# C for a state-space scan in sixteen copies in memory, one for each eight partitions, in a four-layer convolution kernel

## The chip, the core and the metric

The kernel runs on one core of one Trainium2 chip. A core has a matrix engine (PE in the profile, its weight loads shown as PEld), a vector engine (DVE), a scalar engine (ACT), a general engine (POOL) and a queue engine (SP) that here only issues DMAs. Sixteen DMA engines, shared by all queues of the core, move data between the chip's memory and the on-chip memory of 128 partitions (rows). The metric is the time of one launch in device microseconds.

## What is computed

The input is a tensor of 16 images with 192 channels of 64 x 64 points. Four residual layers follow each other, each of the form x = x + layer(groupnorm(x)): an elementwise likelihood model (layer 0), a five-point stencil with a 960-to-192 matrix (layer 1), a selective scan (layer 2), and a depthwise convolution with a batch norm (layer 3). The change is in layer 2:

```python
xs = jnp.stack([xf, xt, xf[..., ::-1], xt[..., ::-1]], axis=1)   # 4 directions k
x_dbl = jnp.einsum('bkdl,kcd->bkcl', xs, x_proj_weight)
dts, Bs, Cs = jnp.split(x_dbl, [R, R + N], axis=2)               # N = 16 states, R = 6
...
def step(h, inp):
    d, u, Bt, Ct = inp
    dA = jnp.exp(d[..., None] * A)
    h = dA * h + (d * u)[..., None] * Bt[:, :, None, :]
    y = jnp.einsum('bkdn,bkn->bkd', h, Ct)
    return (h, y)
```

For each image b, direction k and state n, C is one row of 4096 values, and it multiplies the state of every one of the 192 channels. B is used the same way.

## The kernel before

**Tiles.** Two images make a pair, and a pair's 384 rows (2 x 192 channels) are three tiles j of 128 partitions. Tile 0 holds rows of the first image only, tile 2 rows of the second only, and tile 1, the middle one, 64 rows of each. Eight pairs are worked off one after the other by `pair`: `scans` (layer 2) and then `layer3`. Inside the scans of pair i, the generator `front` does layers 0 and 1 and the projections of layer 2 for pair i+1, a little at each step, on whatever engines have room. The front of the first pair runs alone, before any scan.

**The scan loop.** `scans` runs 768 steps s a pair: over the tiles j, in each over the four directions in the order `ORDER` = (1, 3, 0, 2), in each over four chunks of `LC` = 1024 points, in each over the 16 states n. A step is: PE spreads one row of B over 128 partitions (`spread`), DVE multiplies it by du (`product`), ACT makes dA (`decay`), DVE runs the recurrence (`TENSOR_TENSOR_SCAN` into `h`). Two states share a tile `h`[128, 2048]; after each second step u = s // 2 POOL multiplies that tile by `cb`, the two rows of C spread over all partitions (L1035). After each fourth step POOL also issues a DMA that adds one `h` tile to another (L1037, `h<-h` in the profile), and PE sums the result up over the states (`add_up`). There are five `h` tiles and three `cb` tiles; a scan that opens an `h` tile waits until the DMA and the sums that used it before are done.

**Where C comes from.** `project` makes B, C and dt for chunk c of 512 points. The 128 rows of C are 64 rows for k = 1, 3 (which need their columns and rows exchanged) and 64 for k = 0, 2, and all are written by one DMA into `c_d` (L759). `split` reads the first 64 back into `nat`, ACT exchanges them into `ct` (L830), and one DMA for each m puts `ct` into `cp_d` (L832). `load_c(u)` (L966), called at every second step for the step after the next (L1132), issues the DMA for `cb`: two rows of 1024 values of `c_d` or `cp_d` that lie side by side, read as one row of 8 KB by each of the 128 partitions (L977). For the middle tile it issues two DMAs of 64 partitions each, one for each image.

**Order.** In the scans the instructions stand in the order in which the program issues them (`_InOrder`). SP carries the `cb` loads, all loads and stores of the front, and the loads of B and dt; each of its DMAs signals through one of eight semaphores in turn and first waits for the DMA that had that semaphore before.

Of the kernel before, what the change touches and what calls it, by code (L numbers as in the profile page):

```python
# [22 lines left out]
P = 128  # L23
# [3 lines left out]
L = HW * HW  # L27
# [9 lines left out]
K, N, R = 4, 16, 6  # L37
LC = 1024
NC_ = L // LC
ORDER = (1, 3, 0, 2)  # L40
RD = 2 * R


SUM = 6

# [59 lines left out]
def conv_preact_kernel(ctx: ExitStack, tc: tile.TileContext, a: dict):  # L107
    nc = tc.nc
    x_in = a["x"]
    out = a["out"]  # L110
# [24 lines left out]
    for part in range(3):  # L135
        rows = slice(32 * part, 32 * part + 32)
# [162 lines left out]
    class Made:  # L299
        def __init__(self, n):  # L300
            def d(name, shape, dtype=F32):
                return dram.tile(shape, dtype, name=f"{name}{n}")

            self.x2 = d("x2_d", [NT * P, L])
            self.b = d("b_d", [P, L])
            self.c = d("c_d", [NC_, P, LC])
            self.dt = d("dt_d", [K * RD, L])

            self.bp = d("bp_d", [K, BP, L], BF16)
            self.cp = d("cp_d", [NC_, 2 * 2 * N, LC])  # L310
            self.dtp = d("dtp_d", [2 * RD, L])
            self.gm = const.tile([P, NT], F32, name=f"gm{n}")
            self.rstd = const.tile([P, NT], F32, name=f"rstd{n}")
            self.std = const.tile([P, NT], F32, name=f"std{n}")
# [322 lines left out]
    def layer1(o, E, ps, deep, st, gm, rstd):  # L637
        with tc.tile_pool(name="l1w", bufs=1) as w_, tc.tile_pool(name="l1x", bufs=2) as xk, tc.tile_pool(
# [87 lines left out]
                advance()  # L726
            yield

    def project(o, E, ps):

        with tc.tile_pool(name="pjw", bufs=1) as w_, tc.tile_pool(name="pjx", bufs=3) as xk:
            less = w_.tile([P, NT], F32, name="less")
            E.act.activation(less, o.gm, AF.Copy, scale=-1.0)
            proj = w_.tile([P, NT, 2 * P + K * RD], F32, name="projs")
            E.sp.dma_start(out=proj, in_=a["proj"])
            xns = {}

            def load(c):
                if c < 8:
                    xns[c] = xk.tile([P, NT, 512], F32, name="pj_x")  # L740
                    for j in range(NT):
                        E.sp.dma_start(
                            out=xns[c][:, j, :],
                            in_=row_tiles(o.x2)[:, j, 512 * c : 512 * c + 512],
                        )

            after = []

            def norm(c, j):
                if c < 8:  # L750
                    on_scalar(E, xns[c][:, j, :], xns[c][:, j, :], less, o.rstd, j)

            def done(to, c, m, p):
                yield
                yield
                r = xk.tile([P, 512], F32, name="pj_r", tag="pj_r")[:m]
                E.act.copy(r, p)
                cs = slice(512 * (c % 2), 512 * (c % 2) + 512)
                E.sp.dma_start(  # L759
                    out=to[c // 2, :, cs] if to is o.c else to[:, 512 * c : 512 * c + 512], in_=r  # L760
                )
                yield

            def advance():
                for g in list(after):
                    if next(g, after) is after:
                        after.remove(g)

            load(0)
            load(1)  # L770
            for _ in range(3):
                yield
            for j in range(NT):
                norm(0, j)
                yield
            for c in range(8):
                for at, (to, d0, m) in enumerate(
                    ((o.b, 0, P), (o.c, P, P), (o.dt, 2 * P, K * RD))
                ):
                    p = ps("pj_p")[:m]  # L780
                    for j in range(NT):
                        E.pe.matmul(
                            p, proj[:, j, d0 : d0 + m], xns[c][:, j, :], start=(j == 0), stop=(j == NT - 1)
                        )
                        yield 0.57
                        advance()
                    norm(c + 1, at)
                    after.append(done(to, c, m, p))
                xns.pop(c)
                load(c + 2)  # L790
            while after:
                yield
                advance()
            yield

    def split(o, E):

        with tc.tile_pool(name="sp1", bufs=1) as one, tc.tile_pool(name="sp2", bufs=2) as two:
            nat = one.tile([P, L], F32, name="nat")
            E.sp.dma_start(out=nat[0:64, :], in_=o.b[0:64, :])  # L800
            E.sp.dma_start(
                out=nat[64:128, :].rearrange("p (m l) -> p m l", l=LC),
                in_=o.c[:, 0:64, :].rearrange("m p l -> p m l"),
            )
            bts, dts = {}, {}

            def load(m):
                if m < NC_:
                    bts[m] = two.tile([P, LC], F32, name="bt")
                    E.sp.dma_start(out=bts[m][64:128, :], in_=o.b[64:128, LC * m : LC * m + LC])  # L810

            def load_dt(m):
                if m < NC_:
                    dts[m] = one.tile([2 * RD, LC], F32, name="dtn")
                    E.sp.dma_start(
                        out=dts[m].rearrange("p (h w) -> p h w", w=LC // HW),
                        in_=image(o.dt[: 2 * RD, :])[:, :, 16 * m : 16 * m + 16],
                    )

            load(0)  # L820
            load_dt(0)
            for _ in range(5):
                yield
            for m in range(NC_):
                load(m + 1)
                cs = slice(LC * m, LC * m + LC)
                bt = bts.pop(m)
                ct = one.tile([P, LC], F32, name="ct")
                for rows, to in ((slice(0, 64), bt), (slice(64, 128), ct)):
                    E.act.copy(image(to[rows, :]), columns(nat[rows, :])[:, 16 * m : 16 * m + 16, :])  # L830
                    yield
                E.sp.dma_start(out=o.cp[m], in_=ct[64:128, :])  # L832
                dt = one.tile([2 * RD, LC], F32, name="dtt")
                E.act.copy(image(dt), dts.pop(m).rearrange("p (h w) -> p w h", w=LC // HW))
                yield
                E.sp.dma_start(out=o.dtp[:, cs], in_=dt)
                load_dt(m + 1)
                for part in range(3):
                    h = one.tile([P, LC], BF16, name="part", tag=f"part{part}")
                    E.act.copy(h, bt)  # L840
                    if part < 2:
                        E.gps.tensor_tensor(bt, bt, h, ALU.subtract)
                    yield
                    for at, k in enumerate(ORDER):
                        E.sp.dma_start(
                            out=o.bp[k, 32 * part : 32 * part + 32, cs],
                            in_=h[32 * at : 32 * at + 32, :],
                        )
                yield
# [54 lines left out]
    def scans(i, o, p3, st3, begun, nxt):  # L904

        E = _Engines(tc, True)
        with ExitStack() as es:
# [58 lines left out]
            def load_c(u):  # L966
                t, n = divmod(2 * u, N)
                j, k, at, first = todo[t]
                cb = cbs[u] = cp.tile([P, 2 * LC], F32, name="cb")
                src, row = (o.c, 64 + 16 * k) if k % 2 == 0 else (o.cp, 16 * (k - 1))  # L970
                for b, rows in {
                    0: ((0, slice(0, P)),),
                    1: ((0, slice(0, 64)), (1, slice(64, P))),
                    2: ((1, slice(0, P)),),
                }[j]:
                    r = row + N * b + n
                    two = src[at // LC, r : r + 2, :].rearrange("r l -> (r l)").unsqueeze(0)  # L977
                    E.sp.dma_start(
                        out=cb[rows, :], in_=two.to_broadcast([rows.stop - rows.start, 2 * LC])
                    )  # L980

            def step_rest(t):

# [55 lines left out]
            def add_up(s):  # L1039

                turn = (s - SUM - 3) % 4
                if turn < 2:
                    t, n = divmod(s - SUM - turn, N)
                    if t < 0:
                        return
                    u = (s - SUM - turn) // 2
                    if n == 3 and turn == 0:
# [81 lines left out]
            for s in range(total):  # L1129
                t, n = divmod(s, N)  # L1130
                j, k, at, first = todo[t]
# [37 lines left out]
                if n != 6:  # L1169
                    add_up(s)  # L1170
            for s in range(total, total + SUM + 1):
                add_up(s)
# [133 lines left out]
    with tc.tile_pool(name="fin", bufs=1) as fin, tc.tile_pool(  # L1306
# [7 lines left out]
            out=zs.rearrange("p i j s -> p i (j s)"), in_=zstat_d.rearrange("i p s -> p i s")  # L1314
# [37 lines left out]
        with tc.tile_pool(name="last", bufs=3) as lp:  # L1352
            for i in range(npair):
                for j in range(NT):
                    z = lp.tile([P, L], F32, name="zl")
                    r = lp.tile([P, S, S], F32, name="rl")
# [116 lines left out]
```

## Time and profile before

| | us |
|---|---|
| median of 3 runs (29228.16 to 29253.04) | 29240.98 |
| the profiled execution | 29265.98 |
| its span on the core | 29264.2 |

| engine | busy us | share of the span |
|---|---|---|
| DVE | 23846.3 | 81% |
| PE | 22247.3 | 76% |
| POOL | 20043.6 | 68% |
| ACT | 16341.4 | 56% |

The three tiles of a pair show up as three stretches of about a millisecond each. In the profile, queue q1 carries what SP issues and q0 what POOL issues (the `h<-h` DMAs). "DMA share" is the mean busy share of the 16 DMA engines in a stretch. A wait line names the engine that waited, the tile it was about to write, and what ended the wait.

### The profile page before, as it was taken

To read this page: it belongs to the slowest core of one execution; us is meant where nothing else is said; L and a number is where in the kernel's file an instruction comes from. 1 tells how busy PE (TensorE), PEld (TensorE's weight loads), DVE (VectorE), ACT (ScalarE), POOL (GpSimd) and SP (SyncE) were. 2 spreads that over 40 slices of the span, in tenths; PEclk is the share of its full clock that TensorE was granted. 3 is DMA by queue.
4 is the path that set the end of the run, shared out by engine and by line. 5 is a ranking of instruction groups with operands and counts; after the bars stand their busy time and mean duration, and the time that the engine had idled before them with its cause. 6 is when DMAs were issued, how large, how long until landed. Compare 5 with 4: busy or idle time off the path is not lost. (4 is left out here: it accounts for less than half of the span.)

```text
span 29264.2 us, 182538 instructions
## 1 busy us (share of the span) xinstructions
PE 22247.3 (76%) x51508; PEld 8757.2 (30%) x51508; DVE 23846.3 (81%) x15095; ACT 16341.4 (56%) x23358; POOL 20043.6 (68%) x7266
## 2 busy tenths in 40 slices
PE   9788777877778777787768877787777877766663
PEld 4333323333233332333323332233323333222221
DVE  0388888879888898888988789888888889899994
ACT  7377445763557644775447744477445763534442
POOL 2377766767767776777767777677776777767762
PEclk9898888988888898888889888898888988877776
DMA  3589985899769985899858998589976999579975
GB/s 100 151 237 220 236 243 150 238 214 237 203 194 232 220 236 162 240 231 228 237 156 238 221 233 244 150 240 220 239 220 173 237 219 237 175 200 222 230 213 236
DMA packets 1542949, 6225.84 MB, mean 213 GB/s; under 512 B 486800, under 2 KB 489328, under 8 KB 935216
## 3 DMA queue, kind: packets, MB, share of 16 engines
q1 hardware_dynamic: 1317296, 4543.25, 53.7%
q0 software_dynamic: 221184, 1610.71, 27.3%
q10 hardware_dynamic: 3456, 60.21, 0.5%
q8 instruction: 412, 6.75, 0.1%
q14 instruction: 601, 4.92, 0.1%
HBM read 3859.17 MB, written 340.96 MB: 144 GB/s over the span
## 5 line engine op out<-in xcount | busy, mean ns | idle before, releaser
L66 POOL TENSOR_TENSOR h<-h,cb 128x2048 f32<-128x2048 f32 x3072 | 14037.5, 4573 | 6252.2 <-ACT state L66 5242.4
L66 DVE TENSOR_TENSOR_SCAN h<-dA,state,pbt 128x1024 f32<-128x1024 f32 x4608 | 10808.8, 2346 | 2204.5 <-DMA h<-h 1644.9
L66 DVE TENSOR_TENSOR pbt<-du,pbt 128x1024 f32<-128x1024 f32 x6144 | 7425.6, 1209 | 455.5 <-PE pbt L66 280.6
L66 ACT ACTIVATE dA<-delta,t_alog 128x1024 f32<-128x1024 f32 x6144 | 7041.5, 1147 | 6.5
L66 PE MATMUL ysum<-h,ident 128*128 128x512 f32 x12288 | 6717.0, 675 | 149.6 <-DMA h<-h 149.6
L66 PE MATMUL pbt<-bp,pick 96*128 96x512 bf16 x8192 | 2878.2, 438 | 3561.5 <-DVE h L66 3502.8
L66 ACT COPY state<-h 128x1 f32<-128x1 f32 x6144 | 1149.5, 187 | 7282.0 <-DVE h L66 7262.4
L66 DVE TENSOR_TENSOR_SCAN h<-dA,pbt 128x1024 f32<-128x1024 f32 x1536 | 3508.6, 2284 | 607.2 <-DMA h<-h 420.5
L66 PEld LDWEIGHTS ysum<-h,ident 128*128 128x128 f32 x12288 | 2717.5, 222 | 3390.1 <-issue 3123.0
L66 PE MATMUL p<-m,wms 128*96 128x512 f32 (+1 forms) x5376 | 2980.5, 660 | 58.1 <-ACT lu L66 50.7
L66 PE MATMUL pbt<-bp,pick_mix 96*128 96x512 bf16 x4096 | 1427.6, 435 | 1735.4 <-DVE h L66 1710.8
L66 PEld LDWEIGHTS <-pick 96*128 96x128 bf16 x8192 | 678.8, 103 | 6648.4 <-DVE h L66 4925.1
L66 PE MATMUL l_p<-l_xp,w1s 128*128 128x512 f32 x3920 | 2075.1, 649 | 11.8 <-POOL l_xp L66 11.8
L1234 POOL TENSOR_TENSOR l_g<-l_g,l_m 128x1024 f32<-128x1024 f32 x672 | 1614.7, 2404 | 614.3 <-ACT l_g L1230 455.2
L66 POOL DMA_DIRECT2D h<-h x1536 | 1366.7, 890 | 495.4 <-POOL h L66 456.3
L66 PE MATMUL p<-m,wts 96*128 96x512 f32 x2688 | 1492.7, 672 | 187.1 <-ACT m L66 185.8
L66 PE MATMUL p<-t,wts 96*128 96x512 f32 x2688 | 1477.4, 632 | 0.0
L66 ACT ACTIVATE m<-m,bias,sp 96x512 f32<-96x512 f32 x1344 | 1080.4, 804 | 689.4 <-DMA m<-l_xn 674.1
L66 ACT ACT_TABLE_LOAD x1082 | 1388.2, 1283 | 17.6
L66 PEld LDWEIGHTS <-pick_mix 96*128 96x128 bf16 x4096 | 360.2, 103 | 3295.3 <-DVE h L66 1832.5
L66 PEld LDWEIGHTS p<-m,wms 128*96 128x96 f32 (+1 forms) x5376 | 1043.8, 196 | 952.7 <-issue 433.1
L66 ACT ACTIVATE t<-p,bias 96x512 f32<-96x512 f32 x1344 | 900.4, 682 | 553.8 <-PE p L66 544.2
(249 smaller groups left out, 21451.1 us busy)
## 6 DMA issues: line engine op xcount, KB each, us to landing
h<-h POOLq DMA_DIRECT2D x1536, 1024.0 KB, 11.6
cb<-cp_d SPq DMA_DIRECT2D x1024, 1024.0 KB
cb<-c_d SPq DMA_DIRECT2D x1024, 1024.0 KB
cb<-cp_d SPq DMA_DIRECT2D x1024, 512.0 KB
cb<-c_d SPq DMA_DIRECT2D x1024, 512.0 KB
m<-l_xn SPq DMA_DIRECT2D x3072, 128.0 KB
bp<-bp_d SPq DMA_DIRECT2D x384, 192.0 KB
rl<-x_d ACTq DMA_DIRECT2D x24, 2450.0 KB
```

The costliest lines, as they stand in the source:

```text
L66: return self._tc.keep_in_program_order(call(*args, **kw))
L1234: nc.gpsimd.tensor_tensor(g, g, m, ALU.add)
```

## The change

`c_d` becomes an array [4 chunks, 4 directions, 32, 17 x 1024]: for each chunk and direction 16 copies of the first image's C and then 16 of the second's. A copy is 16 rows of 1024 values and one row of padding that is never written, so copies lie 68 KB apart. `cp_d` is gone: the exchanged rows of k = 1, 3 go straight into their copies. A new `cn_d` holds the rows of k = 1, 3 before the exchange, for `nat` to read.

`copy_c` writes 16 copies of 16 rows (one image, one direction) with one DMA: its source is 16 partitions, each read 16 times, its destination 16 rows x 16 copies. `project` calls it four times for each of 8 chunks of 512 points (k = 0, 2, both images), `split` four times for each of 4 chunks of 1024 (k = 1, 3).

`load_c` issues one DMA in all cases. Its source is 16 consecutive copies, each read eight times, its destination the 128 partitions; for the tiles 0, 1 and 2 it starts at copy 0, 8 and 16, so that the middle tile gets eight copies of each image.

```diff
+COPIES = 16
...
-            self.c = d("c_d", [NC_, P, LC])
+            self.cn = d("cn_d", [P // 2, L])
+            self.c = d("c_d", [NC_, K, 2 * COPIES, (N + 1) * LC])
...
-            self.cp = d("cp_d", [NC_, 2 * 2 * N, LC])
...
+    def copy_c(E, o, m, k, b, rows, at):
+
+        n = rows.shape[1]
+        to = o.c[m, k, COPIES * b : COPIES * b + COPIES, : N * LC]
+        E.sp.dma_start(
+            out=to.rearrange("c (n l) -> n c l", l=LC)[:, :, at : at + n],
+            in_=rows.unsqueeze(1).to_broadcast([N, COPIES, n]),
+        )
...
-                E.sp.dma_start(
-                    out=to[c // 2, :, cs] if to is o.c else to[:, 512 * c : 512 * c + 512], in_=r
-                )
+                cs = slice(512 * c, 512 * c + 512)
+                if to is not o.c:
+                    E.sp.dma_start(out=to[:, cs], in_=r)
+                    yield
+                    return
+                E.sp.dma_start(out=o.cn[:, cs], in_=r[0:64, :])
+                for n, k in enumerate(ORDER[2:]):
+                    for b in range(2):
+                        at = 64 + 32 * n + 16 * b
+                        copy_c(E, o, c // 2, k, b, r[at : at + N, :], 512 * (c % 2))
...
-                E.sp.dma_start(out=o.cp[m], in_=ct[64:128, :])
+                for n, k in enumerate(ORDER[:2]):
+                    for b in range(2):
+                        row = 64 + 32 * n + 16 * b
+                        copy_c(E, o, m, k, b, ct[row : row + N, :], 0)
...
-                src, row = (o.c, 64 + 16 * k) if k % 2 == 0 else (o.cp, 16 * (k - 1))
-                for b, rows in {
-                    0: ((0, slice(0, P)),),
-                    1: ((0, slice(0, 64)), (1, slice(64, P))),
-                    2: ((1, slice(0, P)),),
-                }[j]:
-                    r = row + N * b + n
-                    two = src[at // LC, r : r + 2, :].rearrange("r l -> (r l)").unsqueeze(0)
-                    E.sp.dma_start(
-                        out=cb[rows, :], in_=two.to_broadcast([rows.stop - rows.start, 2 * LC])
-                    )
+                c0 = COPIES // 2 * j
+                rows = o.c[at // LC, k, c0 : c0 + COPIES, n * LC : (n + 2) * LC]
+                E.sp.dma_start(
+                    out=cb,
+                    in_=rows.unsqueeze(1).to_broadcast([COPIES, P // COPIES, 2 * LC]),
+                )
```

More of the change, by code (lines that the diff above doesn't have):

```diff
@@ L757, in done @@
                 E.act.copy(r, p)
-                cs = slice(512 * (c % 2), 512 * (c % 2) + 512)
-                E.sp.dma_start(
-                    out=to[c // 2, :, cs] if to is o.c else to[:, 512 * c : 512 * c + 512], in_=r
-                )
+                cs = slice(512 * c, 512 * c + 512)
[8 more added lines that the diff above has]
+                        copy_c(E, o, c // 2, k, b, r[at : at + N, :], 512 * (c % 2))
                 yield
@@ L800, in split @@
             E.sp.dma_start(out=nat[0:64, :], in_=o.b[0:64, :])
-            E.sp.dma_start(
-                out=nat[64:128, :].rearrange("p (m l) -> p m l", l=LC),
-                in_=o.c[:, 0:64, :].rearrange("m p l -> p m l"),
-            )
+            E.sp.dma_start(out=nat[64:128, :], in_=o.cn)
             bts, dts = {}, {}
@@ L969, in load_c @@
                 cb = cbs[u] = cp.tile([P, 2 * LC], F32, name="cb")
-                src, row = (o.c, 64 + 16 * k) if k % 2 == 0 else (o.cp, 16 * (k - 1))
-                for b, rows in {
-                    0: ((0, slice(0, P)),),
-                    1: ((0, slice(0, 64)), (1, slice(64, P))),
-                    2: ((1, slice(0, P)),),
-                }[j]:
-                    r = row + N * b + n
-                    two = src[at // LC, r : r + 2, :].rearrange("r l -> (r l)").unsqueeze(0)
-                    E.sp.dma_start(
-                        out=cb[rows, :], in_=two.to_broadcast([rows.stop - rows.start, 2 * LC])
-                    )
+                c0 = COPIES // 2 * j
[4 more added lines that the diff above has]
+                )
             def step_rest(t):
```

## The prediction

> **What bounds the kernel now.** First the page's engine totals (DVE busy 81%), then its groups, for what a scan step costs:
>
> ```profile
> L66 POOL TENSOR_TENSOR h<-h,cb 128x2048 f32<-128x2048 f32 x3072 | 14037.5, 4573 | 6252.2 <-ACT state L66 5242.4
> L66 DVE TENSOR_TENSOR_SCAN h<-dA,state,pbt 128x1024 f32<-128x1024 f32 x4608 | 10808.8, 2346 | 2204.5 <-DMA h<-h 1644.9
> L66 DVE TENSOR_TENSOR pbt<-du,pbt 128x1024 f32<-128x1024 f32 x6144 | 7425.6, 1209 | 455.5 <-PE pbt L66 280.6
> ```
>
> A step is 1209 + 2346 = 3.56 us of DVE; 6144 of them are 21.8 ms of the 29.3. DVE sets the pace, and what it loses is mostly one wait: a scan that opens an h tile waits for the accumulating DMA `h<-h`. POOL's multiply by C (first line) waits mainly for the scans and little for `cb`, as the waits of the whole span say (us in total, times, longest):
>
> ```profile
> DVE h L66 <- DMA h<-h: 2065.4, 719, 11.9
> POOL h L66 <- DMA cb<-c_d: 494.6, 115, 13.2
> POOL h L66 <- DMA cb<-cp_d: 258.5, 61, 9.8
> ```
>
> So C's loads matter through the DMA engines that they share with `h<-h`. Stretches of one tile each show that; the columns are bounds, length, busy us of PE, PEld, DVE, ACT, POOL, clock, DMA share, GB/s. The first three are the tiles of the second pair, the last three those of the last pair, which has no front beside it:
>
> ```profile
> 4714.00:5757.00 1043.00, 845.10 (x2011) 334.21 (x2012) 909.54 (x557) 747.50 (x1105) 767.20 (x275) 0.89 0.88 240
> 5757.00:6874.00 1117.00, 867.66 (x2018) 344.27 (x2017) 904.40 (x548) 688.81 (x1008) 790.31 (x289) 0.87 1.00 221
> 6874.00:7876.00 1002.00, 753.55 (x1745) 290.56 (x1743) 910.84 (x564) 470.91 (x681) 733.00 (x254) 0.86 0.88 247
> ...
> 25675.00:26643.00 968.00, 580.21 (x1136) 199.61 (x1136) 887.52 (x518) 402.17 (x588) 673.61 (x208) 0.72 0.80 217
> 26643.00:27567.00 924.00, 574.22 (x1152) 203.35 (x1153) 888.41 (x520) 400.38 (x584) 674.69 (x209) 0.74 1.02 227
> 27567.00:28544.00 977.00, 591.60 (x1163) 208.31 (x1163) 888.40 (x525) 393.98 (x583) 674.79 (x213) 0.72 0.80 215
> ```
>
> In the middle tile the DMA engines are full (1.00) while fewer bytes move. The packet records behind these rows say why. A packet of `cb` is one partition's 8 KB. In tiles 0 and 2 it takes 376 and 388 ns on average, and 58% of them 316 ns or less (smallest 309, 26.5 GB/s on each of 16 engines, all reading one address); in the middle tile, loaded as 64 + 64 partitions, it takes 569. Other DMAs on 64 partitions show the same factor of two: the 16 KB packets of `nat<-b_d` 1247 ns against 611 for full-width loads. `h<-h` packets take 629 to 660 throughout.
>
> **What the change costs and brings.** Profiled execution: 29265.98 us, span 29264.2; the runs' median 29240.98 is 0.1% lower.
>
> (a) *One load for two.* 2048 half loads become 1024 full ones. SP issues shrink (0.45 us each, SP has room: nothing). If the new load ran like the full loads of today, the middle tile would become like tile 0: 1106 us (mean of the first seven pairs' middle stretches) to 1043, 62 us, seven times, −436; the last pair's, 924, would go to 968, +44. That +44 has a reason: the built program's order shows where scans wait for `h<-h`. In the middle tile before, 44 of 64 waits of the first seven pairs, 5 of 64 in the last, stand at states 0, 4, 8, 12 and the others two steps later, which leaves the DMA 7 us more; after, all 64 stand at the early place, as they do in tile 0.
>
> (b) *Is the new load as fast as a full load?* No row has a source of 16 rows read 8 times and 128 partitions to write. Nearest rows: 376 ns (full) and 569 (two halves). [...] I take 569: the copies in memory cannot help a load that already moves 26.5 GB/s an engine.
>
> Its price. Engine time of tile 0 in the second pair, all packets summed over 16 engines, is 913 us; 16384 packets x (569−376) / 16 add 198: floor 1111. From the other side, the wait: early waits in the middle tile cost 142.8 us for 44 (its waits list), 3.25 each; 64 make 208 where tile 0 has 83.6: 1043 + 125 = 1168. I take the middle, 1140, +97. Middle tile: floor 1120, wait 1117 + 65 = 1182, taken 1151, +34. Tile 2 (53 of 64 early, 52 after): floor 882 + 185 = 1067, wait 1002 + 117 = 1119 (52 x 3.25 = 169 where it waits 52 now), taken 1093, +91. That is 222 a pair, 1554 in seven. Last pair: floors, got in the same way, 934, 941, 931; landing of `h<-h` goes from 11.0 us to the 14.5 of its middle tile, 3.5 us at each of 64 early waits: 1192, 1148, 1201 as upper values (the middle one 924 + 64 x 3.5); taken the middle, 1063, 1045, 1066: +305.
>
> (c) *Writing the copies.* Per pair 8 chunks x 4 DMAs of 0.5 MB and 4 x 4 of 1 MB, 32 MB in place of 3 (`c_d`, `cp_d`: about 10 us of engine time, gone). [...] The trace has 128 rows at 87 ns per 2 KB, 32 rows at 124 (`bp_d<-part`), 64 rows at 244 to 300 per 4 KB. By the 32-row price: 2.0 and 4.0 us a DMA, 128 us a pair. [...]
>
> Where it falls: this stage of the front lies in tile 2, with DMA already busy:
>
> ```profile
> 7465.00:7633.00 168.00, 144.67 (x336) 50.60 (x337) 148.61 (x89) 104.48 (x162) 113.21 (x36) 0.95 0.86 258
> 7633.00:7790.00 157.00, 91.50 (x180) 31.83 (x179) 139.39 (x84) 97.42 (x116) 120.67 (x41) 0.71 0.95 265
> 1070.00:1133.00 63.00, 60.30 (x135) 20.96 (x133) 0.00 (x0) 37.33 (x62) 0.00 (x0) 1.00 0.45 150
> 1133.00:1207.00 74.00, 4.26 (x8) 1.36 (x8) 1.47 (x2) 41.76 (x31) 19.98 (x10) 0.50 0.53 128
> ```
>
> 294 of 325 us are used. [...] 294 + 310 − 325 = 279 must come on top; (b)'s extra inside this stretch is counted there. The loads issued ahead absorb some 5 us at each of 12 entries: 220 a pair, 1540 in seven. The first pair's front stands alone (last two rows; nothing hides it): 28 us used of 63 and 39 of 74, so 28+160−63 and 39+160−74: +250.
>
> Sum: 29266 + 1554 + 305 + 1540 + 250 = 32915, taken **32,920 us**. With copies at the low end 294 + 118 − 325 = 87 a pair and +70 at the start: 31,800. With (b) at its wait values (+307 a pair, +672 last) and full (c), 33,900.
>
> **Rivals.** *Loads stay fast, only copies cost.* [...] (a) −436 + 44, (c) 1540 + 250: 30,660. Copies at the low end too: 29,550. Chance 0.22 together.
>
> *Faster.* Sixteen engines reading one address could be what stretches 42% of `cb` packets beyond 316 ns. Then copies bring all to about 309: 69 us less engine time in a tile of 1043, `h<-h` lands sooner, and half its 2065 us of waits go, with (a) about −1300 before (c). It decides as long as the copies add less than some 160 us a pair; at their low end (87 a pair and 70, together 680) it gives 28,650. Against it: DMAs share engines with `h<-h`, which explains stretched packets as well. Chance 0.06.
>
> *No net change*, gains of (a) paying for cheap copies: within 0.2% (what this measurement tells from none), chance 0.02.
>
> Main case 0.70. Range 29,900 to 34,600: it takes in the first rival with full copy cost, and (b) and (c) at both ends. Faster 0.06, same 0.02, slower 0.92.
>
> **What would show it.** `cb` packets near 569 in all tiles, DMA share near 1.0 everywhere, `h<-h` landing at 13 to 14 us where it is 10.7 and 11.0, and DVE's wait for it above 4 ms: (b) right. Share 0.8 to 0.9 in the last pair's tiles with 970 us each: (b) wrong. The stretch from the first `pj_r` to the last `part` twice as long, POOL waiting for `cb` there, the first scan 250 us later: (c) right. If copies run at full rate, 80 us a pair, the sum is wrong by 1.6 ms.

## The result and the profile after

The changed kernel takes 32651.03 us (median of 4 runs, 32630.75 to 32671.76); the kernel before, on the same chip, 29247.01 (29228.16 to 29283.51). The ratio is 1.1162, with a 95% interval of 1.1143 to 1.1182: slower by 3.4 ms. The profiled execution after took 32630.75 us, its span is 32628.6.

The engines do what they did before; what grew is waiting. First the groups of the scan step and then the waits of the whole span, after (busy us, mean ns | idle us before, what ended most of it; in a wait: us in total, times, longest):

```profile
L67 POOL TENSOR_TENSOR h<-h,cb 128x2048 f32<-128x2048 f32 x3072 | 13976.9, 4553 | 9466.3 <-ACT state L67 6706.0
L67 DVE TENSOR_TENSOR_SCAN h<-dA,state,pbt 128x1024 f32<-128x1024 f32 x4608 | 10808.6, 2346 | 4469.5 <-DMA h<-h 3358.6
L67 DVE TENSOR_TENSOR pbt<-du,pbt 128x1024 f32<-128x1024 f32 x6144 | 7425.5, 1209 | 877.4 <-PE pbt L67 502.2
```

```profile
DVE h L67 <- DMA h<-h: 4419.0, 990, 25.8
POOL h L67 <- DMA cb<-c_d: 2470.1, 326, 39.3
```

A scan still takes 2346 ns. DVE's wait for the accumulating DMA went from 2065 to 4419 us, POOL's for `cb` from 494.6 + 258.5 to 2470. Of the 3152 us that were lost after the start of the first scan, DVE's waits hold 3113: 2354 more for `h<-h`, 537 more for ACT's `dA` (88.7 to 625.6) and 222 more for PE's `pbt` (280.6 to 502.2). The last figure also bounds what the lower clock of PE in the rows below can have cost through `pbt`. Next the same six stretches as before the change, one tile each (second pair, last pair; the columns are bounds, length, busy us of PE, PEld, DVE, ACT, POOL, clock, DMA share, GB/s):

```profile
5336.00:6459.00 1123.00, 872.43 (x2020) 342.57 (x2020) 910.24 (x557) 752.85 (x1111) 770.13 (x276) 0.86 0.98 223
6459.00:7568.00 1109.00, 863.50 (x2008) 342.47 (x2008) 903.17 (x546) 682.25 (x1003) 789.23 (x289) 0.87 0.98 223
7568.00:8883.00 1315.00, 783.42 (x1746) 296.99 (x1747) 912.76 (x564) 468.82 (x682) 729.15 (x254) 0.77 0.95 211
28765.00:29808.00 1043.00, 584.22 (x1136) 201.83 (x1136) 887.64 (x519) 402.40 (x589) 672.27 (x208) 0.70 0.92 201
29808.00:30860.00 1052.00, 591.78 (x1152) 205.97 (x1152) 888.27 (x520) 399.81 (x584) 675.90 (x209) 0.71 0.91 202
30860.00:31908.00 1048.00, 591.59 (x1163) 208.24 (x1164) 888.21 (x525) 393.68 (x582) 674.21 (x213) 0.71 0.90 197
```

The DMA engines are now almost full in the tiles of the second pair (0.95 to 0.98, where tiles 0 and 2 had 0.88) and stand at 0.90 to 0.92 in the last (before, 0.80, 1.02 and 0.80), while in every tile but the second pair's middle one they move fewer bytes per second than before. The packet records give the reason: a `cb` packet takes 562 ns on average, and about that in all three tiles (563, 559, 553; before 376, 569, 388). An `h<-h` packet is unchanged (646 against 648 ns), but a whole `h<-h` DMA lands after 13.7 us where it was 11.6.

Where the 3364 us between the two spans arose, from the starts of the scans:

| stretch | before, us | after, us | difference, all pairs |
|---|---|---|---|
| first pair's front, up to the first scan | 1206.8 | 1418.6 | +212 |
| tile 0, mean of seven pairs | 1043.4 | 1133.0 | +627 |
| middle tile, mean of seven | 1105.7 | 1120.6 | +104 |
| tile 2, mean of seven | 1003.7 | 1310.6 | +2148 |
| last pair, three tiles | 2868.9 | 3142.8 | +274 |

They add up to 3365. The layer-3 stretches between the pairs and the end are as they were.

### The profile page after: what moved, and what is told of

It is laid out like the page before. It is cut to its first block, busy times and chain, and to the rows that moved or that the text cites. A ratio compares the mean times of both kernels' runs of the same rounds, so it can differ in the third digit from the quotient of the medians.

```text
span 32628.6 us, 181060 instructions
## 1 busy us (share of the span) xinstructions
PE 22721.5 (70%) x51508; PEld 8881.9 (27%) x51508; DVE 23830.5 (73%) x15095; ACT 16315.2 (50%) x23358; POOL 20025.0 (61%) x7266
## 5 line engine op out<-in xcount | busy, mean ns | idle before, releaser
L67 DVE TENSOR_TENSOR_SCAN h<-dA,state,pbt 128x1024 f32<-128x1024 f32 x4608 | 10808.6, 2346 | 4469.5 <-DMA h<-h 3358.6
L67 DVE TENSOR_TENSOR pbt<-du,pbt 128x1024 f32<-128x1024 f32 x6144 | 7425.5, 1209 | 877.4 <-PE pbt L67 502.2
L67 PE MATMUL pbt<-bp,pick 96*128 96x512 bf16 x8192 | 2980.2, 452 | 4483.1 <-DVE h L67 4378.5
## 6 DMA issues: line engine op xcount, KB each, us to landing
h<-h POOLq DMA_DIRECT2D x1536, 1024.0 KB, 13.7
```

The costliest lines, as they stand in the source:

```text
L67: return self._tc.keep_in_program_order(call(*args, **kw))
```

## The experiments

Two theories for the slow load, and several for the copies, were to be told apart. "Ports" in the expectations is the name of a theory: how long a packet takes depends on the form of a DMA and on the partitions that it touches. No trace shows ports; what the runs show is the time of the packets. "Engine time" below is the sum of all packet times in a stretch over 16 engines, from the packet records. The runs up to the one with even and odd partitions are single ones; nine runs of the kernel before lay within 71 us of each other.

**The shape of the load alone.** The kernel before; only tiles 0 and 2 load in the new shape, from one address.

```diff
+                    if j == 1:
...
+                    else:
+                        E.sp.dma_start(
+                            out=cb,
+                            in_=two.unsqueeze(1).to_broadcast([16, P // 16, 2 * LC]),
+                        )
```

> The kernel before, with one thing of the change: in tiles 0 and 2 the load of C has the new shape, source 16 x 8 x 8 KB, but all 16 groups read one address (step 0). No copies are written; the middle tile keeps its two half loads. Theory 'ports' (the split over the DMA engines makes the load slow, not the place it reads from): cb packets about 560 ns in tiles 0 and 2, tile 0 1043 -> about 1133 us and tile 2 1004 -> about 1094 in the first seven pairs, last pair 968 -> 1043 and 977 -> 1048; total 29,250 + 7 x 180 + 146 = about 30,660 us. Theory 'addresses' (reading 16 copies 68 KB apart is what is slow): packets stay 376 and 388 ns, 29,250 us.

Measured: 30433.26 us against 29272.69 of the kernel before. Tiles 0 and 2 of the second pair and of the last:

```profile
4841.00:5966.00 1125.00, 871.44 (x2020) 342.92 (x2020) 909.50 (x557) 753.56 (x1112) 771.34 (x276) 0.86 0.99 223
7067.00:8141.00 1074.00, 759.73 (x1745) 291.51 (x1743) 911.72 (x564) 471.30 (x681) 732.30 (x254) 0.84 0.99 230
26727.00:27751.00 1024.00, 580.19 (x1136) 199.82 (x1136) 887.57 (x518) 401.94 (x589) 673.44 (x208) 0.71 0.92 205
28683.00:29712.00 1029.00, 591.74 (x1162) 208.67 (x1162) 887.88 (x524) 393.38 (x582) 673.68 (x213) 0.71 0.91 204
```

Nothing is changed but that the source's count of 128 is written as 16 x 8. The share is 0.99 in the second pair, packets take 542 to 569 ns, and tile 0 has, at 1134 us (mean of seven), all of its loss. Tile 2 gets 65 us longer, not 90: of its 122 us of idle DMA time before, 13 are left. The place that the load reads from is not what makes it slow.

**The copies alone.** The kernel after with the loads of before, all from the first copy of an image.

```diff
-                c0 = COPIES // 2 * j
-                rows = o.c[at // LC, k, c0 : c0 + COPIES, n * LC : (n + 2) * LC]
...
+                    two = o.c[at // LC, k, COPIES * b, n * LC : (n + 2) * LC].unsqueeze(0)
+                    E.sp.dma_start(
+                        out=cb[rows, :], in_=two.to_broadcast([rows.stop - rows.start, 2 * LC])
+                    )
```

> The kernel after, with the loads of before (128 partitions, or 64 + 64 in the middle tile, from one address: the first of the sixteen copies). All copies are still written. Theory 'ports': packets of cb 376 ns again, tiles 0 and the middle as before (1043, 1106), tile 2 1004 + 217 = about 1221 us, first scan at about 1419 us, last pair as before; total 29,250 + 7 x 217 + 212 = about 30,980 us. Theory 'together' (the copies hurt mainly because the slow loads have already filled the DMA engines, so that with fast loads they find room): tile 2 below 1100 us, total 29,700 to 30,100.

Measured: 31193.31 us. Packets of `cb` are back at 374 to 394 ns in tiles 0 and 2; tile 2 takes 1241 us (mean of seven, +238), the first scan starts at 1415 us. The second pair's tile 2, and within it the stage that writes the copies, from the first `pj_r` to the last `part`:

```profile
7317.00:8569.00 1252.00, 776.28 (x1746) 294.43 (x1745) 912.27 (x565) 467.73 (x681) 731.48 (x254) 0.79 0.88 223
7909.00:8436.00 527.00, 244.29 (x494) 81.55 (x494) 274.63 (x163) 188.18 (x264) 221.84 (x72) 0.70 0.88 200
```

The stage took 325 us before. Engine time in a tile 2 rose by 213 us (882 to 1095), the tile by 238: "ports" was nearly right on the size, and "together" is out, for the copies cost as much beside fast loads. The two experiments are close to additive: tile 2 gets 65 us longer from the shape and 238 from the copies, 303 of the 307 after.

**The copies from more partitions.** As the last kernel, but one DMA from 64 partitions in place of four from 16 (the layout of `c_d` is turned so that one pattern reaches all rows).

```diff
-                for n, k in enumerate(ORDER[2:]):
-                    for b in range(2):
-                        at = 64 + 32 * n + 16 * b
-                        copy_c(E, o, c // 2, k, b, r[at : at + N, :], 512 * (c % 2))
+                copy_c(E, o, c // 2, 64, r[64:128, :], 512 * (c % 2))
```

> As the kernel with plain loads, but the sixteen copies are written by one DMA from 64 partitions in place of four DMAs from 16 partitions each; the bytes (32 MB a pair), the packet sizes and the stage are the same. [...] Theory 'bytes' (writing 32 MB into memory is the price, whatever the source): as with 16 partitions, tile 2 about 1221, total about 30,980.

Measured: 30476.3 us, between the kernel before and the 31,193 us of the four DMAs from 16 partitions. The same bytes cost less engine time (+151 us in a tile 2 in place of +213, with 12 DMAs a pair where there were 48; the growth of the 2 KB packets' time over the added packets is about 153 ns each where 16 partitions give 199, an estimate), so "bytes" alone is out. The tile grew by 147 us, and the first scan came 124 us later. The cost follows the engine time almost one to one in both kernels; the idle DMA time that the prediction had counted on was not to be had.

**The copies in another queue.** Is that because C's loads stand behind the copies in SP's queue?

```diff
-        E.sp.dma_start(
+        E.act.dma_start(
             out=to.rearrange("c (n l) -> n c l", l=LC)[:, :, at : at + n],
```

> As the kernel with plain loads (31,193 us), but the copies are issued by ACT into its own DMA queue, so that no load of C stands behind a burst of copies in SP's queue. There the copies added 213 us of engine time to a tile 2 (packets of all queues over 16 engines, 882 -> 1095 us), and the tile grew by 238 us (1004 -> 1241), though it had 122 us of idle DMA time before. Theory 'order' (the loads stand behind the bursts, so the idle time cannot be used): POOL's wait for cb in the stage, 145 us of 527, falls below 50, tile 2 goes to 1100 to 1150 us, the total to 30,200 to 30,600 us. Theory 'engine time' (the engines themselves are the limit in this stage, in whatever order): tile 2 stays at 1200 or more, total 30,900 to 31,300 us.

Measured: 30958.43 us; tile 2 takes 1212 us. The wait of POOL in this stage of the second pair's tile 2, first with the copies in SP's queue, then in ACT's:

```profile
POOL h L67 <- DMA cb<-c_d: 145.5, 8, 35.5
```

```profile
POOL h L67 <- DMA cb<-c_d: 124.8, 11, 30.4
```

POOL waits nearly as long, and the tile gets only 29 of its 238 us back. But the run does not separate order from engine time. SP's queue holds the loads of x for `project` as well, and ACT's wait for them over the whole span, first with the copies in SP's queue, then in ACT's, nearly vanishes:

```profile
ACT pj_x L67 <- DMA pj_x<-x_d: 814.1, 42, 28.1
```

```profile
ACT pj_x L67 <- DMA pj_x<-x_d: 17.5, 15, 2.5
```

In its place ACT now stands before the same instruction for 380.1 us and before `dtt` for 270.9 us with nothing to wait for that the profile shows, behind its issues of copies, which may hide a late x. Engine time still fits the sizes (+197 us in a tile 2, which grew by 209), but that it is the cause of the rest is not shown: a queue that holds up neither the loads nor ACT was not tried.

**Many addresses.** The kernel before with one plain load of 128 partitions in every tile, each partition from another address.

```diff
+                rows = o.c.rearrange("m (g r) l -> (m g) (r l)", r=2)
+                E.sp.dma_start(out=cb, in_=rows[P * (u % 2) : P * (u % 2) + P, :])
```

> The kernel before, with one plain 128-partition load in all tiles, each partition reading another 8 KB of C (128 addresses). It leaves out the right choice of rows: every step multiplies by other rows of C. Theory 'ports': packets as for today's full loads, about 376 ns in all three tiles; middle tile 1106 -> 1043, last pair's middle 924 -> 968; total 29,250 - 436 + 44 = about 28,860 us. Theory 'addresses': 560 ns or more in all tiles, about 30,800 us. The third, that sixteen engines reading one address is what stretches today's packets: about 309 ns, tiles below 1000 us, total under 28,500.

Measured: 28785.09 us. Packets take 373 to 394 ns in all three tiles of the first seven pairs, just as from one address. So neither does one shared address stretch packets, nor do many addresses help or harm a plain load. It also shows what one load with such packets in the middle tile is worth: 1106 to 1027 us in the first seven pairs, but 924 to 983 in the last.

**The middle tile's halves on two queues.**

```diff
-                    E.sp.dma_start(
+                    (E.act if rows.start else E.sp).dma_start(
                         out=cb[rows, :], in_=two.to_broadcast([rows.stop - rows.start, 2 * LC])
```

> The kernel before; the middle tile's second half load (partitions 64 to 127) is issued by ACT into its own queue, beside the first half in SP's. [...] If the 16 engines stay in step, so that all write one half at a time: packets 569, total 29,250 us; and if ACT's issues come late or hold up its exponentials, above 29,400 us.

Measured: 29626.1 us. Packets of the middle tile stay at 564 to 586 ns in SP's queue (mean 555 in ACT's), and the tile takes 1139 us. Two queues do not speed up the halves' packets. The longer tile is not the second queue's cost alone: of the waits for `h<-h` that the trace shows in the second pair's middle tile, 57 of 58 stand at states 0, 4, 8, 12, where it was 41 of 57 before.

**Even and odd partitions.** The same two half loads, to every second partition.

```diff
-                    1: ((0, slice(0, 64)), (1, slice(64, P))),
+                    1: ((0, slice(0, P, 2)), (1, slice(1, P, 2))),
```

> The kernel before; in the middle tile the two half loads go to the even and to the odd partitions in place of the lower and the upper 64. Same count, bytes, sources and places in the queue. It leaves out the arrangement of the data that belongs to it, so half of the rows of that tile are multiplied by the other image's C. [...] Theory 'halves' (two DMAs of 64 partitions are slow because they are two, or of 64): packets 569, total 29,250 us.

Measured: 28578.88 us. The middle tile's packets fall from 569 ns to between 377 and 382, and the tile from 1106 to 1009 us. Same bytes, count, sources and queue; only which partitions a load writes differs. "Halves" is out. The choice of partitions does not explain the slow load of the change, though, which writes all 128 too. No record tells which engine moved a packet, so how a load is split over the engines is not seen, and why the 16 x 8 form is slow (562 ns a packet after, 542 to 569 in the first experiment) stays open; that the form is the cause is shown.

This run and the one with many addresses also weigh the place of the wait. Their packets differ little (397 and 425 ns in the last pair's middle tile), but with one load a step the scans that wait for `h<-h` stand early in all 54 cases that the trace shows there, with two in 4 of 49. The last pair's middle tile and its wait, one load first, then two:

```profile
26101.00:27084.00 983.00, 587.86 (x1152) 202.96 (x1152) 888.31 (x520) 399.60 (x585) 676.02 (x209) 0.72 0.81 217
```

```profile
DVE h L66 <- DMA h<-h: 70.3, 34, 4.1
```

```profile
25955.00:26878.00 923.00, 571.55 (x1152) 202.97 (x1153) 888.73 (x522) 400.55 (x585) 676.18 (x209) 0.74 0.82 227
```

```profile
DVE h L66 <- DMA h<-h: 2.4, 2, 1.5
```

The DMA share is nearly the same; 60 us lie between the two, and the wait fell from 70.3 to 2.4 us. A whole `h<-h` DMA lands there after 11.5 and 10.9 us (medians); 0.6 us off each of the 34 waits would be some 20 us (an estimate), so the place is the larger part.

**A whole kernel with interleaved images.** If the rows of the middle tile alternate between the images, even and odd halves serve the right rows.

```diff
-    pick_mix = const.tile([BP, N, 2, 64], BF16, name="pick_mix")
+    pick_mix = const.tile([BP, N, 64, 2], BF16, name="pick_mix")
...
+                        for b in range(2):
+                            E.sp.dma_start(out=xrs[c, j][b::2, :], in_=v[64 * b : 64 * b + 64])
...
+                    1: ((0, slice(0, P, 2)), (1, slice(1, P, 2))),
...
+MIXED = np.arange(2 * C)
+MIXED[P : 2 * P] = MIXED[P : 2 * P].reshape(2, 64).T.reshape(-1)
```

> A whole kernel on the pattern of even and odd partitions: the rows of the middle tile alternate between the two images from the output of layer 1 on (weights and constants permuted in their layout, one more matrix for the group norms, loaded three times a pair; layer 1's residual and the last output of that tile moved by two DMAs of every second partition). C is stored and loaded as before. Theory 'ports': as the run with even and odd partitions, about 28,700 us, plus up to 60 us for the loads of the matrix: 28,650 to 28,800, ratio to before about 0.982. Theory 'halves': 29,250 to 29,350 us.

Measured: 28678.1 us (5 runs), ratio 0.9799 to the kernel before, interval 0.9785 to 0.9812. The middle tile takes 1013 us. The stretches between the pairs are 13 us longer (355.6 against 342.8 after the first pair), about 90 in all and more than the 60 allowed. There the matrix for the norms is loaded, and the middle tile's output leaves by two DMAs; which of them costs it was not measured.

**Two half loads in every tile.** The place of the wait, used on purpose.

```diff
+                for h in range(2):
+                    r = row + N * (h if j == 1 else j // 2) + n
+                    two = src[at // LC, r : r + 2, :].rearrange("r l -> (r l)").unsqueeze(0)
+                    E.sp.dma_start(out=cb[h::2, :], in_=two.to_broadcast([64, 2 * LC]))
```

> As the kernel with interleaved images (28,678 us), but tiles 0 and 2 also load C by two DMAs, to the even and to the odd partitions, both from the one image. [...] Theory 'place of the wait' (two DMAs a step move it, and a later wait leaves the DMA 7 us more): with even and odd partitions the last pair's middle tile, late, took 923 us, with one full load, early, 983 at the same packets; so the last pair's tiles 0 and 2 go 964 -> about 920 and 974 -> about 925, tile 2 of the first seven pairs 996 -> about 965, tile 0 1047 -> about 1040; total about 28,330 us. Theory 'packets' (only the packets count, the place of the wait does not): 28,680 us, or more by SP's second issue.

Measured: 28258.6 us (5 runs), ratio 0.9659, interval 0.9645 to 0.9672. The last pair's tiles take 920.5, 921.7 and 920.6 us, tiles 0 and 2 of the first seven 1031 and 971. Its tile 2 in the second pair, and the wait of the whole span with interleaved images and one load in tiles 0 and 2, then with two everywhere:

```profile
6608.00:7580.00 972.00, 745.22 (x1745) 287.57 (x1743) 911.22 (x564) 461.84 (x674) 730.48 (x254) 0.87 0.89 251
```

```profile
DVE h L66 <- DMA h<-h: 1430.5, 646, 7.5
```

```profile
DVE h L66 <- DMA h<-h: 920.4, 413, 7.4
```

The wait is below half of the 2065 us before the change. Packets are a little shorter than with one load (374 to 381 ns in tile 2 of the first seven pairs, against 389 to 396; 390 against 426 in the last pair's tile 0). That is too little: in this last tile 0 `h<-h` lands after 10.7 us in place of 11.1, at most 16 us over its 39 waits (an estimate), and the wait fell from 52.0 us to none and the tile by 43. "Packets" alone is out. This is the fastest of the kernels run: 1.0 ms under the kernel before, and 4.4 ms under the one after.

## Why the prediction was right

The forecast was 32,920 us, the result 32,651; the sum of the terms was 3649 us and came to 3365.

| term of the prediction | predicted | measured |
|---|---|---|
| tile 0, (b) | 97 a pair | 90 |
| middle tile, (a) and (b) | 34 | 15 |
| tile 2, (b) and (c) | 91 + 220 | 307 (alone: 65 and 238) |
| last pair | 305 | 274 |
| first front, (c) | 250 | 212 |

**(b), the load is not a full load.** Right in what happens and nearly in size. Packets "near 569 in all tiles" came out at 562, the first experiment puts it on the shape, and there the loss goes to DVE as forecast: of 1161 us, its wait for `h<-h` has 1098. Why the shape is slow is not shown; the 569 was the author's choice between two rows, 376 and 569 ns, neither of which has this shape. In the sums, values midway between a floor of engine time and a price for early waits were taken. Where the engines are nearly full, the tiles end close to the floor: 1120 was the middle tile's and it took 1121, tile 0 had 1111 and took 1133, tile 2 had 1067 and took 1069 in the first experiment. So the price of 3.25 us for each early wait was too large there. It was too large in the last pair as well: the wait of its tile 0 grew by 62 us (53.6 to 115.8), about 1 us for each of 64 early waits where 3.5 were set, and `h<-h` landed after 13.4 us, not 14.5. The sum of 305 there came near 274 because the middle of two limits was taken, not because either was met; that is luck.

**(a), one load for two.** The prediction's condition was not met, but the experiment with many addresses meets it: 1106 went to 1027 (predicted 1043), and 924 to 983 (predicted 968). The odd half of that, that a faster load makes the last pair slower since scans wait earlier, is shown by the 983 against 923 us, most of it by the place.

**(c), the copies.** The signs came: the stage takes 551 us in the second pair (325 before; twice was forecast), and POOL waits 216.8 us for `cb` in it. The size a pair was right, 220 against 238, by two errors that cancel. The 310 us of engine time in a tile, and with it the 160 in each stretch of the first front, is an estimate of the author's that no run shows; in a tile it measured 213. In ACT's queue, where the copies stand alone, a packet of 2 KB takes 172 ns and one of 4 KB 443 on average, where 310 us on top of the old stores' 10 would be about 310 and 620 (8192 packets of 2 KB and 4096 of 4 KB a pair over 16 engines, an estimate) and the 32-row price is 125 and 250: the measurement lies between the two. But of it the prediction let 31 us fall into idle engines and 60 be absorbed by loads issued ahead, and nothing was absorbed. The path, POOL's wait for `cb`, was half right. With the copies alone, DVE's wait for `h<-h` grew by 899 us over the span; its waits for `dA` and `pbt`, which the prediction had at nothing, grew by 480 and 286. In the timeline of the kernel after, while chunks of `project` are copied:

```profile
8302.89 0.72 ACT L67 ACTIVATE pj_x<-pj_x,less 128x512 f32<-128x512 f32 x1 [17.69 <-DMA pj_x<-x_d]
...
8304.36 1.14 ACT L67 ACTIVATE dA<-delta,t_alog 128x1024 f32<-128x1024 f32 x1
...
8305.59 2.35 DVE L67 TENSOR_TENSOR_SCAN h<-dA,state,pbt 128x1024 f32<-128x1024 f32 x1 [9.76 <-ACT dA L67]
```

ACT, in program order, stands 17.7 us before the next chunk of x, whose load stands in SP's queue with the copies; the exponential behind it is late, and the scan waits 9.8 us for it. DVE's wait for `dA` over the span, before and after:

```profile
DVE h L66 <- ACT dA L66: 88.7, 218, 5.0
```

```profile
DVE h L67 <- ACT dA L67: 625.6, 182, 15.4
```

**The rivals.** "Loads stay fast" fell with the packets; its sum, 30,660, stands beside 31,193 for the kernel that is just that. "Faster" assumed that one shared address stretches packets, and 128 addresses leave them at 373 to 394 ns. Two side sums of the prediction are off and enter only the low end and a rival: the low end's start is +58 by its own formula (28+64−63 and 39+64−74), not +70, and half of the waits with (a) make about −1425, not −1300.

**Left open.** In the last pair, where nothing is copied, tiles 0 and 2 take 1043 and 1048 us after, but 1024 and 1029 with the same shape and one address; packets are 582 to 585 ns against 568 and 569. Sixteen addresses seem to cost a little in this shape; why is open. No run has a load that reads sixteen copies with packets near 380 ns. Whether the copies cost what they do through engine time, through the order in a queue or through ACT is not settled either.

## What to carry to other kernels

Before a load is rebuilt, sum its packets' times and ask which partitions each DMA writes together: here a load with packets of 376 to 388 ns from one address kept them from 128 (373 to 394), and one with 569 was mended by choosing other partitions (every second one, 377 to 382), not by copying its source. Beside engines that were almost full (busy 294 of 325 us in that stage), new transfers cost about their engine time (213 and 238 us, 151 and 147, 197 and 209), in either queue, and they reached the bounding engine also through another one that waits in order for its data (ACT 17.7 us for a chunk of x, then the scan 9.8 us for ACT). After a wait for a DMA has been found, look at where in the program it stands as well as at how long the DMA takes: two steps later, this one had nearly vanished (70.3 to 2.4 us in the last pair's middle tile).

## What the runs showed of the hardware

- A broadcast load of 128 partitions in the pattern 16 x 8 takes 542 to 569 ns per 8 KB packet, in the pattern 128 it takes 376 and 388 (tiles 0 and 2 before), from one address in both.
- 64 partitions that lie side by side take 569 ns a packet, every second of 128 takes 377 to 382, in loads that are otherwise the same.
- Two queues for two half loads did not shorten the packets (564 to 586 ns in SP's queue, mean 555 in ACT's).
- Writing each row to 16 places in memory from 16 partitions took 172 ns for a packet of 2 KB where the copies have a queue of their own; beside C's loads it comes to about 199 from 16 partitions and 153 from 64 (estimates, as above); full-width stores of the kernel before show 87.
- An `h<-h` packet of 8 KB takes 646 to 648 ns on average before and after the change, about twice the 309 of the fastest `cb` packets.
